# Cross-attention with heads of 64: products of 32 columns in place of 64, and the place of one weight in its pool

## The chip, the cores and the metric

The kernel runs on one core of a Trainium2 chip. The metric is device time in microseconds of one execution. Before the change three runs took 1196.61, 1198.14 and 1200.52 us: the median is 1198.14.

A core has a matrix engine (TensorE, here PE), three engines for elementwise work (VectorE or DVE, ScalarE or ACT, GpSimd or POOL), SyncE (SP), which mostly issues DMAs, and 16 DMA engines. Each engine runs its own instructions in order; semaphores order them among each other. A matmul takes a stationary operand (the "weights" that PE loads) and streams a moving one past it; it can be told to use the whole array of 128 rows by 128 columns, or a part of it. When only 64 or 32 columns are written, a 128-column product is issued as two or four matmuls[...].

## The reference

A decoder of two layers in fp32, on eight entries of 256 tokens with 256 features. The first layer is self-attention, cross-attention with heads of 16, and experts with Sinkhorn routing; the second is self-attention, a cross-attention with a null key and value, and experts with token routing beside a shared expert. The change lies in the second layer's cross-attention. For each of eight entries b it computes, with 16 heads of 64 and a context of 256 tokens of 512 features:

```
q = norm(x) Wq            k, v = ctx Wkv
e = exp(q k / 8)          n = exp(q null_k / 8)
out = (e v + n null_v) / (sum e + n)  Wo
x   = x + norm(out)
```

After it the routed experts need scores, which are one more product of the normed rows, with a router of 8 columns (E = 8). The shared expert is a gated feed-forward network: its first and third weights (`ws13`) make the hidden layer, its second (`ws2`) brings it back.

## The kernel before

Two helpers make a 128x128 block of a product: `product` (line 274) as two matmuls of 64 columns, `product4` (line 280) as four of 32 (`HP` is 32, `XD` 64, `P` 128). `product4` was in use in the first layer and in self-attention, whose heads are 16 wide. Each fp32 matmul shows as two MATMUL and two LDWEIGHTS records in the profile. All row and column forms are written there as rows x columns, so `128*64` is a matmul of 128 rows and 64 columns.

The second cross-attention (`null_cross_attention`, from line 1288) is a loop over b, about 59 us for each entry, from about 486 to 971 us of the span. The body of b first works through the attention itself (`weighted`): for pairs of 128-feature blocks, two heads to a block, scores `stx` (line 1431, 64 rows x 128 columns), their exponential `pTx` on ACT, and a sum of its two halves, `both`, on POOL (line 1437). PE takes the sums over the context with a 0/1 matrix (`den`, line 1446, 32 columns) and the weighted values `ox` (line 1470, 64 columns). The order on PE is: scores of the next pair, `den` of the pair before, `ox` of this one.

Then the projections of entry b+1 are made. Keys, values and queries (`k7`, `v7`, `q7` in `seven`, line 1346 on) are each a 2x2 block product in seven in place of eight multiplications, with sums of weights and rows made on DVE. For the first entry, the queries come from plain products (`features`, line 1293). Their steps are interleaved by hand, in the tuple of generators at line 1607, with the last sums of b (`rest`), the division by the sums (`reciprocals`, which goes through DRAM by SP's queue as `rd` and `rs`; `divide`), and the output product of b (`outward`, line 1529: `wo` and two norms). Then come the routing scores of b-1 (`sc`, `routed_scores`, line 1203) and the null key of b+1 (`nps`, line 1415). The norm of b+1 and of b-1's routed rows (`lnmv`, `lnve`, `lnrs`, `xn`, `xne`) runs on DVE and POOL, and their transposes on PE (line 291).

PE's order is written by hand from the projections on; the order on DVE, ACT and POOL is decided by a scheduler as the program is built.

The last entry (b = 7) has no next one. It closes the pool of the cross-attention's weights and opens a pool `mids` in the same place, on the right side of SBUF, for the shared expert: `load_shared` (line 1054) places `ws13`, two hidden buffers, then `ws2` from the lowest address up. `ended` (line 1033) sets the unused rows of a buffer's last part to zero on POOL. SP issues the load of `ws13` (lines 1028 and 1029, `ws<-L_ffn_ws_DF`) and later that of `ws2` (lines 1039 and 1040, `ws<-L_ffn_ws_FD`), and PE starts the shared expert's hidden products `hx` (line 1079) in the places where the projections stood before.

The routed experts (`token_experts`, from 971 us) use `product` for their hidden layer and output.

Of the kernel before, what the change touches and what calls it, by code (L numbers as in the profile page):

```python
# [29 lines left out]
F32 = mybir.dt.float32  # L30
# [9 lines left out]
P = 128  # L40
B, S, D = 8, 256, 256
NT = B * S // P
H, HD = 16, 16
HP = 32
CTX = 512
XH, XD = 16, 64
# [4 lines left out]
NFC = len(FCH)  # L51
# [106 lines left out]
def plain(  # L158
# [119 lines left out]
        ]  # L278

    def product4(out, lhsT, rhs, start, stop):  # L280
        for h in range(0, P, HP):
            nc.tensor.matmul(  # L282
                out[h : h + HP], lhsT[:, h : h + HP], rhs, start=start, stop=stop, skip_group_check=True
            )

    def transposed(rows, work, mm, tag, dst=None, bufs=2):

# [492 lines left out]
    nc8 = XH // 2  # L780
# [244 lines left out]
    def w_in(pool, src1, src3, name):  # L1025

        t = pool.tile([P, 2, 2 * FF + tail], F32, name=name, tag=name)
        nc.sync.dma_start(t[:, :, :FF], src1.rearrange("(c p) f -> p c f", p=P))
        nc.sync.dma_start(t[:, :, FF + tail :], src3.rearrange("(c p) f -> p c f", p=P))
        nc.gpsimd.tensor_copy(t[:, :, FF : FF + tail], t[:, :, 2 * FF :])  # L1030
        return t

    def ended(t):

        nc.gpsimd.memset(t[tail:, full, :], 0.0)
        return t
# [10 lines left out]
    shared = {}  # L1047
# [5 lines left out]

    def load_shared(pool):

        shared["ws13"] = w_in(pool, a["L1_ffn_ws1_DF"], a["L1_ffn_ws3_DF"], "ws13")

        shared["mid_s"] = [ended(pool.tile([P, NFC, 2 * S], F32, name=f"mid{i}")) for i in range(2)]
        shared["ws2"] = ended(pool.tile([P, NFC, D], F32, name="ws2"))

    def hidden(mid, first, n, pair, silu):

# [139 lines left out]
    def routed_scores(b):  # L1202

        ps = mm.tile([P, 2, D], F32, tag="mm", name="sc")
        for t in range(2):
            for c in range(2):
                product(
                    ps[:, t, :E], shared["xnT"][:, c, bass.ts(2 * b + t, P)], shared["router"][:, c, :], c == 0, c == 1
                )
        nc.vector.tensor_copy(sc[:, 2 * b : 2 * b + 2, :], ps[:, :, :E])  # L1210
# [77 lines left out]
    def null_cross_attention(phase):  # L1288
# [4 lines left out]
        def features(dst, w, rows, copy):  # L1293
            n = w.shape[1]
            for c2 in range(0, nc8, 2):
                ps = mm.tile([P, 2, S], F32, tag="mm", name="fm")
                for i in range(2):
                    for cc in range(n):
                        product(
                            ps[:, i, :], w[:, cc, (c2 + i) * P : (c2 + i + 1) * P], rows[:, cc, :], cc == 0, cc == n - 1  # L1300
                        )
                copy(dst[:, c2 : c2 + 2, :], ps)
# [43 lines left out]
        def seven(name, s_terms, t_terms, dst, tokens_first):  # L1346

            n = t_terms[0].shape[1]
            xy = scp.tile([P, 2, 2 * S], F32, tag="sc", name=name)
            xb, yb = xy[:, 0], xy[:, 1]  # L1350

            read = {id(xb): [], id(yb): []}

            def reads(bank, ins):
                read[id(bank)].append(ins)
                return ins

            def product_of(which, bank, fresh):

                s, t = s_terms[which - 1], t_terms[which - 1]  # L1360
                for i in range(1 if tokens_first else 4):
                    for c in range(n):
                        if tokens_first:
                            args = bank, s[:, c, :], t[:, c, :]
                        else:
                            args = bank[:, bass.ts(i, P)], t[:, c, bass.ts(i, P)], s[:, c, :]
                        for made in product(*args, fresh and i == 0 and c == 0, c == n - 1):
                            for other in (xb, yb):
                                for ins in read[id(other)] if other is not bank else ():
                                    tc.declare_no_dep(made.ins, ins.ins, reason="another bank")  # L1370

            if tokens_first:

                def of(i, j):
                    return dst[:, i, 8 * j : 8 * j + 8, :]

                def seen(bank):
                    return bank.rearrange("p (h d) -> p h d", h=8)

            else:  # L1380

                def of(i, j):
                    return dst[:, 4 * j : 4 * j + 4, bass.ts(i, P)]

                def seen(bank):
                    return bank.rearrange("p (c t) -> p c t", c=4)

            def kept(bank, what):
                t = work.tile([P, 2 * S], F32, tag="pT", name=f"{name}{what}", bufs=4)
                reads(bank, nc.scalar.copy(t, bank))  # L1390
                return seen(t)

            product_of(1, xb, True)
            p1 = kept(xb, "p")
            yield
            zb = mm.tile([P, 2 * S], F32, tag="mm", name=f"{name}z")
            product_of(2, zb, True)
            nc.vector.tensor_tensor(of(0, 0), p1, seen(zb), ALU.add)
            product_of(5, yb, True)
            p5 = kept(yb, "v")  # L1400
            yield
            product_of(6, xb, False)
            u = kept(xb, "u")
            yield
            product_of(7, xb, False)
            reads(xb, nc.vector.tensor_tensor(of(1, 1), p5, seen(xb), ALU.add))
            yield
            product_of(3, yb, False)
            reads(yb, nc.vector.tensor_tensor(of(0, 1), u, seen(yb), ALU.add))
            yield  # L1410
            product_of(4, xb, False)
            nc.scalar.copy(of(1, 0), seen(xb))
            yield

        def null_key(xnT):
            nps = mm.tile([P, 2, S], F32, tag="mm", name="nps")
            for k in range(2):
                product(nps[:, 0, :], wn[:, k].rearrange("p g w -> p (g w)"), xnT[:, k, :], k == 0, k == 1)
            en = work.tile([P, S], F32, tag="en", name="en")
            nc.scalar.activation(en, nps[:, 0, :], AF.Exp, scale=scale)  # L1420
            return en

        def weighted(kT, v, qT):
# [36 lines left out]
            for c2 in range(0, nc8, 2):  # L1460
                now = ahead
                if c2 + 2 < nc8:
                    ahead = block(c2 + 2)
                for i, both in enumerate(before):
                    sums(c2 - 2 + i, both)
                o = mm.tile([P, 2, S], F32, tag="mm", name="ox")
                for i, (pT, _) in enumerate(now):
                    for kt in range(2):
                        for g in range(2):
                            nc.tensor.matmul(  # L1470
                                o[XD * g : XD * (g + 1), i, :],
                                v[:, kt, 2 * (c2 + i) + g, :],
                                pT[:, g, kt, :],
                                start=kt == 0,
                                stop=kt == 1,
                                skip_group_check=True,
                            )
                (nc.vector.tensor_copy if c2 % 4 else nc.scalar.copy)(oT[:, c2 : c2 + 2, :], o)
                before = [both for _, both in now]
# [49 lines left out]
        def outward(b, oT, en):  # L1529
            y = work.tile([P, 2, D], F32, tag="y", name="yx", bufs=1)  # L1530
            ps = mm.tile([P, 2, D], F32, tag="mm", name="wo")
            for t in range(2):
                cols = bass.ts(t, P)
                product(ps[:, t, :], en[:, cols], nvw, True, False)
                for c in range(nc8):
                    product(ps[:, t, :], oT[:, c, cols], wout_x[:, c, :], False, c == nc8 - 1)
            nc.scalar.copy(y, ps)
            mv, rs = norm_stats([y[:, t, :] for t in range(2)], 1e-6, small, "lx")
            for t in range(2):
                xt = x[:, 2 * b + t, :]  # L1540
                normed(y[:, t, :], y[:, t, :], mv, rs, t)
                nc.vector.tensor_tensor(y[:, t, :], y[:, t, :], lns, ALU.mult)
                nc.vector.tensor_tensor(y[:, t, :], y[:, t, :], lnb, ALU.add)
                nc.gpsimd.tensor_tensor(xt, xt, y[:, t, :], ALU.add)
# [17 lines left out]
        en = null_key(xnT)  # L1562
# [5 lines left out]
        for b in range(B):  # L1568
# [31 lines left out]
            if b == 1:  # L1600
                in_range()
            if not more:
                w_out(shared["ws2"], a["L1_ffn_ws2_FD"])
                routing_tables(late)
            if more:

# [1251 lines left out]
```

## Time and profile before

| | us |
|---|---|
| three runs | 1196.61, 1198.14, 1200.52 |
| profiled execution, its own time | 1198.71 |
| its span | 1197.0 |
| PE busy / PE's weight loads | 1135.5 / 706.5 |
| DVE / ACT / POOL busy | 566.2 / 447.5 / 417.6 |
| `ox`, PE busy (512 records) | 62.3 |
| `wo`, PE busy (512 records) | 58.0 |
| `den`, PE busy (256 records) | 21.3 |

The span is the profiled execution from its first to its last instruction. Busy times of an engine add up the durations of its instructions; PE's weight loads are shown apart, since they overlap matmuls. [...] how long a group really holds PE is seen from its start to the start of the next group. A number in brackets at the end of a timeline's line is idle time before the group, and what ended it. PEclk is the clock that PE was granted, where 1.00 is full speed.

### The profile page before, as it was taken

Reading aid. Unit: us, or ns where it says so; the run is one execution under the profiler, and the core shown is the slowest. Engines: PE = TensorE matmul, PEld = TensorE weight load, DVE = VectorE, ACT = ScalarE, POOL = GpSimd, SP = SyncE. Lnnn points to the kernel's source line nnn. Section 1 sums busy time; section 2 is a strip of 40 time slices with the busy share of each in tenths; the row PEclk is TensorE's granted clock in tenths of the full one; section 3 lists DMA queues with packets and bytes.
Section 4 is the critical chain, followed back from the end, with each engine's and each line's share of the span. In section 5 each row is a group of like instructions: output and inputs, shape, how many; then the busy total and the mean of one; then the engine's idle time right before and its main releaser. Section 6 shows DMA issues by size and latency. Waiting matters only on the chain.

```text
span 1197.0 us, 31939 instructions
## 1 busy us (share of the span) xinstructions
PE 1135.5 (95%) x13788; PEld 706.5 (59%) x13788; DVE 566.2 (47%) x1564; ACT 447.5 (37%) x696; POOL 417.6 (35%) x482
## 2 busy tenths in 40 slices
PE   6898899998899999999999999999998999999996
PEld 2334444454445454666676767666664576888864
DVE  5465878778685643824241424242324473222213
ACT  3666665665443541314141414141413230222220
POOL 3245365455655730314141414141415114100013
PEclk9999999999999999999999999999998999999999
DMA  7046232130200600020202010101103007799924
GB/s 226 1 133 204 91 119 92 54 122 2 84 2 17 233 3 19 2 54 2 54 2 54 6 50 10 46 19 37 24 15 105 5 30 305 277 414 394 392 73 129
DMA packets 51446, 116.78 MB, mean 98 GB/s; under 512 B 8272, under 2 KB 36416, under 8 KB 46944
## 3 DMA queue, kind: packets, MB, share of 16 engines
q1 hardware_dynamic: 45120, 98.90, 24.0%
q0 software_dynamic: 3456, 12.73, 2.9%
q10 hardware_dynamic: 2720, 3.02, 0.7%
q8 instruction: 110, 1.80, 0.6%
q14 instruction: 40, 0.33, 0.1%
HBM read 104.00 MB, written 27.93 MB: 110 GB/s over the span
## 4 chain that ended last, share of the span: by engine, by line
PE 76%; POOL 7%; issue 6%; DVE 6%; ACT 4%; DMA 1%; SPq 0%; POOLq 0%; ACTq 0%; DVEq 0%
PE h L276 7%; PE k L276 6%; PE v L276 6%; PE wo L276 5%; PE ox L1470 5%; PE stx L1431 5%; PE st L334 4%; PE out L1846 4%; PE o L371 3%; PE out L1663 3%; PE h L1079 3%; PE qk L282 3%; PE q L276 3%; ACT pT L345 2%; PE den L1446 2%
## 5 line engine op out<-in xcount | busy, mean ns | idle before, releaser
L345 ACT ACTIVATE pT<-st 128x1024 f32<-128x1024 f32 (+1 forms) x128 | 110.7, 919 | 64.3 <-PE st L334 64.3
L371 PE MATMUL o<-pT,padv 128*32 128x256 f32 (+1 forms) x1536 | 99.7, 370 | 4.3 <-POOL pT L350 4.2
L371 PEld LDWEIGHTS o<-pT,padv 128*32 128x32 f32 x1536 | 40.6, 109 | 86.2 <-issue 37.5
L1437 POOL TENSOR_TENSOR both<-pTx 128x512 f32<-128x512 f32 x64 | 81.2, 1296 | 29.0 <-ACT pTx L1435 23.8
L276 PE MATMUL h<-xrT,w 128*64 128x128 f32 (+1 forms) x1936 | 87.0, 250 | 0.4 <-issue 0.4
L276 PEld LDWEIGHTS h<-xrT,w 128*64 128x64 f32 x1936 | 84.4, 137 | 3.3 <-issue 1.1
L345 ACT ACTIVATE pT<-st,kbias 128x1024 f32<-128x1024 f32 x64 | 67.9, 1112 | 44.0 <-PE st L334 44.0
L258 POOL TENSOR_TENSOR lnrs<-lnve,mhalf 128x2 f32<-128x2 f32 x48 | 34.7, 723 | 127.8 <-DVE lnve L256 124.1
L1072 DVE TENSOR_TENSOR midr<-sl,h 128x128 f32<-128x128 f32 x102 | 29.4, 288 | 102.5 <-PE h L276 69.9
L1435 ACT ACTIVATE pTx<-stx 128x1024 f32<-128x1024 f32 x64 | 62.1, 1022 | 40.8 <-PE stx L1431 27.7
L1071 ACT ACTIVATE sl<-h 128x128 f32<-128x128 f32 (+1 forms) x114 | 35.4, 311 | 94.7 <-PE h L276 55.7
L334 PE MATMUL st<-qm,kT 32*128 32x512 f32 (+1 forms) x512 | 66.8, 591 | 4.0 <-ACT pT L345 2.0
L1431 PE MATMUL stx<-qTx,kTx 64*128 64x256 f32 x512 | 64.4, 391 | 2.5 <-ACT pTx L1435 2.5
L282 PE MATMUL qk<-l_wqkv,xnT 128*32 128x512 f32 x512 | 63.3, 607 | 0.7 <-ACT xnT L294 0.7
L1470 PE MATMUL ox<-pTx,vx 128*64 128x256 f32 x512 | 62.3, 385 | 0.0
L258 POOL TENSOR_TENSOR lxrs<-lxve,mhalf 128x2 f32<-128x2 f32 x8 | 5.6, 706 | 159.9 <-DVE sc L1210 124.2
L1525 POOL TENSOR_TENSOR oT<-oT,rs 128x512 f32<-128x512 f32 x30 | 37.3, 1273 | 65.0 <-DMA rs<-rd 65.0
L1431 PEld LDWEIGHTS stx<-qTx,kTx 64*128 64x128 f32 x512 | 46.1, 186 | 20.3 <-ACT pTx L1435 7.2
L276 PE MATMUL wo<-wout_x,oT 128*64 128x256 f32 x512 | 58.0, 379 | 0.0
L350 POOL TENSOR_SCALAR_AFFINE_SELECT pT<-pT 128x512 f32<-128x512 f32 x64 | 42.0, 670 | 41.8 <-ACT pT L345 38.7
L1846 PE MATMUL out<-w,midr 128*64 128x256 f32 x408 | 47.1, 379 | 2.7 <-issue 2.7
L1470 PEld LDWEIGHTS ox<-pTx,vx 128*64 128x64 f32 x512 | 33.9, 136 | 26.4 <-issue 12.5
(361 smaller groups left out, 2164.1 us busy)
## 6 DMA issues: line engine op xcount, KB each, us to landing
w<-packs SPq DMA_DIRECT2D x22, 1408.0 KB
w<-packs SPq DMA_DIRECT2D x22, 768.0 KB
rs<-rd SPq DMA_DIRECT2D x16, 512.0 KB
packs<-L_ffn_w_eDF SPq DMA_DIRECT2D x8, 704.0 KB
packs<-L_ffn_w_eDF SPq DMA_DIRECT2D x8, 640.0 KB
packs<-L_ffn_w_eFD SPq DMA_DIRECT2D x8, 640.0 KB
ctxT<-ctx_T SPq DMA_DIRECT2D x8, 512.0 KB
wkv_x<-L_xattn_Wkv POOLq DMA_DIRECT2D x1, 4096.0 KB
```

What stands on the lines that cost most here:

```text
L258: nc.gpsimd.tensor_tensor(rs[:, :n], ve[:, :n], mhalf[:, :n], ALU.pow)
L276: nc.tensor.matmul(out[h], lhsT[:, h], rhs, start=start, stop=stop, skip_group_check=True)
L282: nc.tensor.matmul(out[h : h + HP], lhsT[:, h : h + HP], rhs, start=start, stop=stop, skip_group_check=True)
L334: nc.tensor.matmul(st[:, r, :, :n], self.kT[rows, c, bass.ts(kt, P)], self.qm[rows, :, c, q0:], start=True, stop=True,)
L345: nc.scalar.activation(pT[:, :, :, :n], st[:, 2 * k : 2 * k + 2, :, :n], AF.Exp, scale=self.scale, **kb)
L350: nc.gpsimd.affine_select(out=pT[:, :, :, :P], in_=pT[:, :, :, :P], compare_op=ALU.is_ge, fill=0.0, base=0, pattern=[[0, 2], [0, 2], [1, P ...
L371: nc.tensor.matmul(o[HP * j : HP * j + HP, m, q0:], self.v_pad[:, kt, 8 * c + 2 * j + m, :], pTs[j // 2][:, j % 2, m, : S - q0], start=kt ...
L1431: nc.tensor.matmul(st[:, g, kt, :], kT[rows, c, bass.ts(kt, P)], qT[rows, c, :], start=True, stop=True)
L1435: nc.scalar.activation(pT, st, AF.Exp, scale=scale)
L1437: nc.gpsimd.tensor_tensor(both, pT[:, :, 0, :], pT[:, :, 1, :], ALU.add)
L1470: nc.tensor.matmul(o[XD * g : XD * (g + 1), i, :], v[:, kt, 2 * (c2 + i) + g, :], pT[:, g, kt, :], start=kt == 0, stop=kt == 1, skip_group ...
L1846: nc.tensor.matmul(ps[h], mid[:, i, h], sets[k % len(sets)][1][:, i, :], start=i == 0, stop=i == NFC - 1, skip_group_check=True,)
```

## The change

`product4` returns the list of its matmuls, as `product` did. `product4` replaces `product` in the second cross-attention: in `features`, in the seven products of keys, values and queries, in the null key, in `outward`, and in `routed_scores`. The weighted values `ox` are issued as four matmuls of 32 columns where they were two of 64. `product` stays for the routed experts. Apart from that, `ws2` is taken first in the pool `mids`, so that it is at the lowest address and `ws13` above it; the `ended` for `ws2` moves from its allocation to just ahead of its load. Lines from 282 on are two higher afterwards.

```diff
     def product4(out, lhsT, rhs, start, stop):
-        for h in range(0, P, HP):
+        return [
             nc.tensor.matmul(
                 out[h : h + HP], lhsT[:, h : h + HP], rhs, start=start, stop=stop, skip_group_check=True
             )
+            for h in range(0, P, HP)
+        ]
...
     def load_shared(pool):
+        shared["ws2"] = pool.tile([P, NFC, D], F32, name="ws2")
         shared["ws13"] = w_in(pool, a["L1_ffn_ws1_DF"], a["L1_ffn_ws3_DF"], "ws13")
         shared["mid_s"] = [ended(pool.tile([P, NFC, 2 * S], F32, name=f"mid{i}")) for i in range(2)]
-        shared["ws2"] = ended(pool.tile([P, NFC, D], F32, name="ws2"))
...
     def routed_scores
-                product(
+                product4(
                     ps[:, t, :E], shared["xnT"][:, c, bass.ts(2 * b + t, P)], shared["router"][:, c, :], c == 0, c == 1
...
         def features
-                        product(
+                        product4(
...
         def seven, product_of
-                        for made in product(*args, fresh and i == 0 and c == 0, c == n - 1):
+                        for made in product4(*args, fresh and i == 0 and c == 0, c == n - 1):
...
         def null_key
-                product(nps[:, 0, :], wn[:, k].rearrange("p g w -> p (g w)"), xnT[:, k, :], k == 0, k == 1)
+                product4(nps[:, 0, :], wn[:, k].rearrange("p g w -> p (g w)"), xnT[:, k, :], k == 0, k == 1)
...
         def weighted
-                        for g in range(2):
+                        for at in range(0, P, HP):
                             nc.tensor.matmul(
-                                o[XD * g : XD * (g + 1), i, :],
-                                v[:, kt, 2 * (c2 + i) + g, :],
-                                pT[:, g, kt, :],
+                                o[at : at + HP, i, :],
+                                v[:, kt, 2 * (c2 + i) + at // XD, at % XD : at % XD + HP],
+                                pT[:, at // XD, kt, :],
...
         def outward
-                product(ps[:, t, :], en[:, cols], nvw, True, False)
+                product4(ps[:, t, :], en[:, cols], nvw, True, False)
                 for c in range(nc8):
-                    product(ps[:, t, :], oT[:, c, cols], wout_x[:, c, :], False, c == nc8 - 1)
+                    product4(ps[:, t, :], oT[:, c, cols], wout_x[:, c, :], False, c == nc8 - 1)
...
             if not more:
-                w_out(shared["ws2"], a["L1_ffn_ws2_FD"])
+                w_out(ended(shared["ws2"]), a["L1_ffn_ws2_FD"])
```

## The prediction

> **What bounds the kernel now.** I read first the busy time of each engine and the chain that ended last, on the profile's page:
>
> ```profile
> PE 1135.5 (95%) x13788; PEld 706.5 (59%) x13788; DVE 566.2 (47%) x1564; ACT 447.5 (37%) x696; POOL 417.6 (35%) x482
> ...
> PE 76%; POOL 7%; issue 6%; DVE 6%; ACT 4%; DMA 1%; SPq 0%; POOLq 0%; ACTq 0%; DVEq 0%
> ```
>
> TensorE is the bound. An average hides stages, so next came the windows: one cross-attention entry (b=2), then a stretch of the last one. Columns: window, length, busy time (instructions) of PE, PEld, DVE, ACT, POOL, granted clock, DMA share, GB/s.
>
> ```profile
> 605.00:664.00 59.00, 58.68 (x658) 40.03 (x658) 20.03 (x51) 17.90 (x27) 19.40 (x21) 1.00 0.11 28
> 919.90:926.50 6.60, 6.52 (x8) 2.52 (x8) 3.03 (x6) 0.00 (x0) 0.29 (x1) 0.54 0.93 261
> ```
>
> In the stage that the change edits PE is all but never free, at full clock; a microsecond taken out of PE's stream there is a microsecond of the end. But "busy" includes what a matmul loses at its start, so I measured starts against starts in the timeline of PE (start, busy time, line, operands, number):
>
> ```profile
> 611.39 1.95 PE L1470 MATMUL ox<-pTx,vx 128*64 128x256 f32 x16
> 613.27 2.00 PE L1431 MATMUL stx<-qTx,kTx 64*128 64x256 f32 x16
> 615.19 0.64 PE L1446 MATMUL den<-both,hot 128*32 128x256 f32 x8
> 615.76 1.95 PE L1470 MATMUL ox<-pTx,vx 128*64 128x256 f32 x16
> 617.64 0.64 PE L1446 MATMUL den<-both,hot 128*32 128x256 f32 x8
> ...
> 621.11 1.97 PE L276 MATMUL k<-ctxT,wkv_x 128*64 128x128 f32 x32
> 623.01 0.64 PE L1446 MATMUL den<-both,hot 128*32 128x256 f32 x8
> 623.58 1.97 PE L276 MATMUL k7z<-ctxT,wkv_x 128*64 128x128 f32 x32
> 625.37 1.81 PE L276 MATMUL k<-sw,tw 128*64 128x128 f32 x30
> ```
>
> The same timeline of the earlier cross-attention, which already works in 32 columns:
>
> ```profile
> 439.45 3.64 PE L282 MATMUL fm<-ctxT,wkv_x 128*32 128x256 f32 x64
> 443.01 0.71 PE L334 MATMUL st<-qm,kT 32*128 32x256 f32 x8
> ...
> 444.55 1.05 PE L282 MATMUL ao<-l_wo,attT 128*32 128x256 f32 x16
> 445.41 3.64 PE L282 MATMUL fm<-ctxT,wkv_x 128*32 128x256 f32 x64
> 448.86 0.62 PE L371 MATMUL o<-pT,padv 128*32 128x128 f32 x16
> 449.30 1.05 PE L282 MATMUL ao<-l_wo,attT 128*32 128x256 f32 x16
> ```
>
> Inside one shape: 64 columns of 256 take 0.108 us a record (`wo`: 3.45 for 32), of 128 0.0546 (`k`: 1.75 for 32). In 32 columns, 256 take 0.0539 (`ao`: 445.41 - 444.55 = 0.86 for 16; `fm`: 448.86 - 445.41 = 3.45 for 64), 128 take 0.0275 (`o`: 0.44 for 16). A 128x128 product is half as many records of twice the length: same time. Where the shape changes it isn't: `ox` then `stx` or `den` is 1.88 where 16 x 0.108 = 1.73 is due, +0.15; `den` then `ox` 0.57 where 8 x 0.0539 = 0.43 is due, +0.14; `k` then `den` 1.90 for 1.75, +0.15; `den` then `k7z` +0.14. From 32 columns to 32 rows, `fm` then `st`, 3.56 for 3.45: +0.11. From 32 to 32 columns: nothing.
>
> [...] here 32 records of `lg` (32 columns of 8) take 0.27 us, 8.6 ns each[...] the window above shows 0.54 after 3.42 us of idleness. [...] the trace has 1.69 us for two `xne` beside POOL's `both`, 0.74 with POOL idle.
>
> **The change part by part.** (1) `ox`, the seven products `k7`, `v7`, `q7`, `wo`, the null key and `fm` of b=0 go to 32 columns: twice the records, each half as long, 0 in themselves; the number of waits in the instructions is the same. (2) What goes is the shape changes against `den`, which is 32 wide. In each b: `den` then `ox` three times, `ox` then `den` once, `k` then `den` once, `den` then `k7z` once: 6 x 0.145 = 0.87. Three `ox` then `stx`, and transposes, stay, at 0.11 for 0.15: 0.11. The first `k7z` group itself takes 1.79 for 1.75: 0.04. (3) `sc`: 16 records of 64 columns of 8 take 0.55 us (start to start, 600.11 to 600.66); at the 8.6 ns of `lg`, 32 take 0.27: 0.28, in each b from 1 on (b-1's scores).
>
> Sum for an entry: 0.87 + 0.11 + 0.04 + 0.28 = 1.30.
>
> (4) What eats it. Sc copies and the last norm chain shift in DVE's order, and from b=1 to 5 POOL takes `lnrs`, `lnrs`, then `both`, where before it took `lnrs`, `both`, `lnrs`, `both`. The first `den` of b=2 already started late: it needs the second `both`, which ended at 610.76 (POOL: `lnrs` to 607.45, `both` to 608.70, `lnrs` to 609.55, `both` to 610.76). With the new order, `lnrs` ends about 606.7, the two `xne` with POOL idle 0.75, `lnve` 0.16, `lnrs` 0.70, two `both` 2.5: 610.8. So this `den` stays where it was, and of the 0.40 saved ahead of it (0.28 at `sc`, some 0.12 at the smaller shape changes), I count half as lost to a wait for `both`: 1.1 for b=2 to 5 (4.4), 0.9 for b=1, where the order changes too, 1.0 for b=0 (no `sc`). b=6 keeps POOL's order: 1.29; b=7 about 1.2. Total 0.9 + 1.0 + 4.4 + 1.3 + 1.2 = 8.8 us.
>
> Costed at nothing, with cover: faster `ox` asks sooner for `pTx` and `both`, which have over 1 us of slack in the middle of an entry; PE's total wait on `pTx` from 486 to 900 is 2.2 us. `oT`'s last division by the sums ends at 639.6 and `wo` reads it at 649.7: 10 us. The 32-wide weight loads run beside matmuls (PEld 40.03 of 59.00). The routed experts keep 64 columns.
>
> (5) `ws2` lowest in its pool. The last entry shows the wait that it might concern:
>
> ```profile
> 915.49 0.40 SPq L1028 DMA_DIRECT2D ws<-L_ffn_ws_DF  x1
> ...
> 919.98 6.62 PE L1079 MATMUL hx<-xnTe,ws 128*128 128x512 f32 x8 [3.42 <-DMA ws<-L_ffn_ws_DF]
> ```
>
> The load of `ws13` leaves right after the last `ox` (914.80), and PE waits for it 3.42 us, then runs 8 records in 6.55 where 8 x 0.43 = 3.43 is due: 3.1 more through the clock. By the addresses, `ws13` overlapped `vx`, which `ox` reads; afterwards `ws2` does, and `ws13` lies on `wkv_x` alone. But in both built programs the wait of `ws13`'s load is still on the last `ox`: the pool's first writer takes on the waits of the pools closed before it. SP's queue behind it (`rd`, `ws2`, `rs`) has the same order. I take 0. Both ends: 0, and -6.5 if it does leave early. What does move is the phase: the wait ends at the transfer's landing, which follows the last `ox` whatever came before, so PE's 3.42 stays.
>
> The profiled execution took 1198.71 us around a span of 1197.0; less 8.8 that is 1189.9 around 1188.2. It lies 0.6 above the median of the runs (1198.14), so the median should be 1189.3; I say 1189.5.
>
> **Rivals.** *A, the other side: narrow records hit a floor.* `k7` and `q7`, with 128 elements a record, leave 27.3 ns per 32-wide record. For: 64-wide records of 64 elements (`h`, 176 in 5.13 us) come no faster than 29.1 ns; if a record, and not the width of its weights, sets that, each loses 1.8 ns: 672 per b, 7 times, 4704 x 1.8 = 8.5 us, and the time is about 1198, no change. At 31 ns it is 17 us: 1206, slower. It decides the sign from about 29.2 ns on. Against: `o` runs 27.5 ns, `lg` 8.6 ns, both 32-wide, though in bursts of 16 and 32 only; 64-wide `sc` shows 59 ns for each pair of columns' loads, so `h`'s floor is that of a 64-wide load.
> *B, POOL late.* If the two `xne` still meet `both` (1.69 instead of 0.75) the first `den` of b=2 to 5 is 0.95 later: -3.8 of the gain, 1193. [...]
> *C, `ws13` leaves early after all*: 6.5 more, 1183. Against: the built waits.
> *D, no cost at the shape changes, only modelled ends*: then nothing is gained, 1198; against it, differences of starts, which aren't modelled, show it.
>
> **How the numbers follow.** Main case 0.66 (1186 to 1193: 8.8 give or take three, as the slow-clock stretch and the runs' spread of 1196.61 to 1200.52 move it). A without change 0.08, A slower 0.07, B 0.10, C 0.06, D 0.03. 0.3% is 3.6 us, about what a measurement of this kernel can tell from no change: faster below 1194.5, slower above 1201.7. Faster: main, C, most of B: 0.80; same: D, most of A's first part and the rest of B: 0.12; slower: A's second part and a little of its first: 0.08. The range from 1184 to 1198.5 holds the main case but for its tails (0.62), B, most of A without change and D (0.10), and is cut through C: some 0.84. Cases of both signs don't share it evenly; the main case's own range stands above.
>
> **What would show it.** Right: `den` to `ox` 0.43, `ox` to `den` and `k` to `den` 1.73 to 1.76, `sc` 0.27, entries near 58.0 instead of 59.1 us, PE still waiting 3.4 us at the last entry's `hx`. Wrong: `k` groups over 1.8 us (A); the first `den` later than before against its own `stx`, on POOL's `both` (B); `ws` landing before the last `ox` (C).

## The result and the profile after

The changed kernel takes 1201.59 us (median of 8 runs, 1198.66 to 1203.56) against 1197.38 for the kernel before in the same comparison: a ratio of 1.0031, 95% interval 1.002 to 1.0042. It is slower by some 4 us, where 8.8 us less was forecast. The profiled execution took 1203.56 around a span of 1201.8; it is the slowest of the eight, so stages are compared below, not spans.

The profile after, from its page: busy times, the chain that ended last, and the queue that brings instructions.

```profile
PE 1133.2 (94%) x17876; PEld 708.3 (59%) x17876; DVE 560.8 (47%) x1564; ACT 447.8 (37%) x696; POOL 418.6 (35%) x482
...
q8 instruction: 142, 2.33, 0.8%
...
PE 71%; POOL 9%; DVE 7%; issue 7%; ACT 4%; DMA 1%; SPq 0%; POOLq 0%; DVEq 0%; ACTq 0%
```

PE is busy for 2.3 us less while the span is longer: PE waits more. `issue`, time in which an engine waited for nothing that the profile shows, went from 6% of the chain to 7%. The line in the middle counts packets, MB and share of time. Before the change it read:

```profile
q8 instruction: 110, 1.80, 0.6%
```

PE's 8,176 additional records came in 32 additional fetches: 0.53 MB / 32 = 16 KB, some 256 records for each. Such a packet of 256 instructions is called a page below.

The windows show where PE waits (columns as in the prediction): the first entry, then b=3, of the kernel after.

```profile
486.00:545.00 59.00, 57.10 (x1172) 38.87 (x1164) 26.96 (x45) 16.56 (x23) 17.36 (x14) 1.00 0.12 29
663.00:722.00 59.00, 57.26 (x1160) 40.13 (x1152) 17.96 (x47) 17.98 (x26) 19.67 (x20) 1.00 0.12 30
```

Before, PE was busy for 58.36 and 58.68 us of these. The clock is at full speed in both. PE's waits from 486 to 990 us, in the view of waits (total, times, longest, in us), after:

```profile
PE k L282 <- issue: 6.4, 6, 1.8
PE hx L1081 <- DMA ws<-L_ffn_ws_DF: 3.5, 1, 3.5
PE stx L1433 <- ACT pTx L1437: 2.5, 8, 0.3
PE q L282 <- DVE qTx L1408: 0.4, 1, 0.4
```

The first line is new; the wait at `hx` is as long as before (3.4). The six waits are inside groups of key products, and PE's timeline shows one:

```profile
515.45 1.93 PE L282 MATMUL k<-sw,wkv_x 128*32 128x128 f32 x64
517.20 1.49 PE L282 MATMUL k<-ctxT,tw 128*32 128x128 f32 x47
519.93 0.73 PE L282 MATMUL k<-ctxT,tw 128*32 128x128 f32 x17 [1.24 <-issue]
520.39 1.99 PE L282 MATMUL v7z<-wkv_x,ctxT 128*32 128x512 f32 x16
```

Between the 47th and the 48th record of one group, with no semaphore between them, 1.51 us pass from start to start where 0.027 is normal. All six together, from start to start, are 7.9 us too long: 1.49, 2.02, 1.49, 0.73, 1.17 and 0.99 in b=0, 1, 3, 4, 5 and 6. b=2 has none. Counted in all records of PE, weight loads and the sequencer's own among them, the restarts stand 2304, 4864, 2304, 2560 and 2304 apart: 9, 19, 9, 10 and 9 x 256. PE stops at the ends of its pages.

What keeps the page away is seen in the DMA queues. From 512.2 to 517.2 us and in the 2 us after it, with packets, MB and share:

```profile
q1 hardware_dynamic: 155, 1.05, 94.2%
```

```profile
q8 instruction: 1, 0.02, 3.8%
q1 hardware_dynamic: 5, 0.00, 0.3%
```

The first 5 us are the two transfers `rs<-rd`, 512 KB each; no instruction packet begins in them. The page that ran out at 518.4 lasted 3.5 us of `k` (128 pairs of a weight load and a matmul at 27.3 ns), so PE entered it near 514.9, in the middle of `rs<-rd`. By the trace's packets, the fetch before had begun at 510.35, 0.2 us after PE entered a page. The next one, due near 515, began only at 517.28, some 2.4 us after PE had entered its page, behind `rs<-rd`, and PE went on at 519.93, 2.65 us after that. For the six stalls, the fetch began 2.1 to 2.8 us after PE entered the page, and from its start to PE's next record 2.61 to 2.92 us passed. A page of `k` lasts 3.5 us, so by these numbers a fetch can start no more than 0.6 to 0.9 us late before PE runs dry. At 64 columns a page of `k` lasts 7.0 us (128 pairs at 54.6 ns), and PE did not stop.

### The profile page after: what moved, and what is told of

Read it like the earlier page. It is cut to its first block, busy times and chain, and to the rows that moved or that the text cites. A ratio compares the mean times of both kernels' runs of the same rounds, so it can differ in the third digit from the quotient of the medians.

```text
span 1201.8 us, 40110 instructions
## 1 busy us (share of the span) xinstructions
PE 1133.2 (94%) x17876; PEld 708.3 (59%) x17876; DVE 560.8 (47%) x1564; ACT 447.8 (37%) x696; POOL 418.6 (35%) x482
## 4 chain that ended last, share of the span: by engine, by line
PE 71%; POOL 9%; DVE 7%; issue 7%; ACT 4%; DMA 1%; SPq 0%; POOLq 0%; DVEq 0%; ACTq 0%
PE v L282 7%; PE h L276 7%; PE k L282 6%; PE wo L282 5%; PE ox L1472 4%; PE st L336 4%; PE out L1848 4%; PE o L373 3%; PE h L1081 3%; PE out L1665 3%; PE qk L282 3%; PE stx L1433 3%; ACT pT L347 2%; PE q L282 2%; PE fm L282 2%
## 5 line engine op out<-in xcount | busy, mean ns | idle before, releaser
L1472 PE MATMUL ox<-pTx,vx 128*32 128x256 f32 x1024 | 63.0, 380 | 0.0
L282 PE MATMUL wo<-wout_x,oT 128*32 128x256 f32 x1024 | 58.2, 379 | 0.0
L1480 DVE COPY oT<-ox 128x512 f32<-128x512 f32 x16 | 11.1, 691 | 81.2 <-PE ox L1472 81.2
```

The costliest lines, as they stand in the source:

```text
L282: nc.tensor.matmul(out[h : h + HP], lhsT[:, h : h + HP], rhs, start=start, stop=stop, skip_group_check=True)
L1472: nc.tensor.matmul(o[at : at + HP, i, :], v[:, kt, 2 * (c2 + i) + at // XD, at % XD : at % XD + HP], pT[:, at // XD, kt, :], start=kt == 0 ...
```

## The experiments

The theory after the result (F): instructions for narrow products are fetched too late, because their fetch waits behind `rs<-rd`. The rival (R): records of 128 elements in 32 columns run dry by themselves. A third part (P, Q) concerns what else is missing from the gain. Beside the time, each run gives the length of seven entries, from the first `stx` of b=0 to that of b=7. The start and the end of the kernel don't enter it: the profiled executions differ by 2.3 us (475.38 and 477.66) when the first null key begins, and up to there the code is the same. The seven entries took 413.01 before and 417.02 after: +4.0 of the 4.2 by which the medians differ. The kernel before was timed again beside each group of runs (medians from 1197.38 to 1198.87), so the ratios compare better than the times. Stalls are counted in the one execution that was profiled.

| run | us | ratio to before, 95% | seven entries, us | stalls in `k`, us |
|---|---|---|---|---|
| changed kernel | 1201.59 | 1.0031 (1.0020 to 1.0042) | 417.02 | 7.9 |
| rs_late | 1193.01 | 0.9955 (0.9939 to 0.9971) | 408.73 | 0 |
| before_rs_late | 1198.91 | 1.0003 (0.9991 to 1.0015) | 412.98 | 0 |
| before_ox32 | 1193.15 | 0.9960 (0.9948 to 0.9973) | 408.89 | 0 |
| no_ws2 | 1199.60 | 1.0017 (1.0004 to 1.0031) | 415.90 | 6.8 |
| late_pool | 1190.78 | 0.9925 (0.9900 to 0.9950) | 405.89 | 0 |
| late_pool_q | 1188.88 | 0.9917 (0.9897 to 0.9937) | 404.03 | 0 |
| rs_twice | 1202.87 | 1.0040 (1.0026 to 1.0054) | 416.05 | 7.0 |
| before_sc32 | 1197.08 | 0.9988 (0.9978 to 0.9998) | 412.80 | 0 |
| page_shift | 1201.99 | 1.0038 (1.0018 to 1.0059) | 414.37 | 5.4 |
| rs_ahead | 1217.78 | 1.0157 (1.0132 to 1.0183) | 433.31 | 15.5 |
| before_seven32 | 1206.42 | 1.0072 (1.0049 to 1.0096) | 419.76 | 5.7 |
| before_pool_q | 1197.63 | 0.9994 (0.9980 to 1.0008) | 411.00 | 0 |

**The transfer out of the way.** In `reciprocals`, the two `rs<-rd` move into a function, `spread`, that is called later, behind a copy of one element:

```diff
-                for made in (k7, k7, v7, k7, k7, k7, v7, v7, q7, v7, q7, v7, v7, q7):
+                for n, made in enumerate((k7, k7, v7, k7, k7, k7, v7, v7, q7, v7, q7, v7, v7, q7)):
                     next(made)
+                    if n == 4:
+                        nc.vector.tensor_copy(rs[:1, 0, :1], kT[:1, 4, :1])
+                        spread()
...
```

> The changed kernel, but the two transfers `rs<-rd` (512 KB each) of b=0 to 6 leave only after the sixth of the seven key products has been added (one VectorE copy of a single element from kT into rs ahead of them). Theory F (fetch): PE's next page of instructions waits behind `rs<-rd`; the stalls of 1.5, 2.0, 1.5, 0.7, 1.2 and 1.0 us in the k groups go, 7.9 us in all: near 1193.7, faster than before. Rival R (a rate): narrow matmuls of 128 elements run dry by themselves, whatever is being transferred: stalls stay, near 1201.6. A slip of the output product `wo` behind the later division would show as a wait of `wo` on POOL or DVE: not expected, 10 us of slack against some 4 us of delay.

> The kernel before, with the same delay of `rs<-rd`. Theory F: at 64 columns a page of instructions lasts twice as long and no fetch was late, so nothing is won: within 1 us of before. If the delay itself is worth something or costs something (another order on VectorE, the later division), it shows here: rival R gives no number of its own, also 0.

The six stalls are gone, and the time is 1193.01, 0.7 us below what F said; R falls. The same group in PE's timeline, with the late transfer:

```profile
517.30 1.93 PE L282 MATMUL k<-ctxT,tw 128*32 128x128 f32 x64
519.05 1.90 PE L282 MATMUL v7z<-wkv_x,ctxT 128*32 128x512 f32 x16
```

It wasn't done quite as written. The copy holds back only the half of `rs` with its element; in b=0 one transfer still ran near 513 to 515.5, and the other from 519 on. The fetch that fell into the first began at 515.81, some 0.8 us after PE had entered its page near 515.0, and that was early enough, in keeping with the 0.6 to 0.9 us above. So half of the transfer at the old time does no harm, which F allows and hadn't said. In the kernel before, the delay brings nothing: 412.98 for seven entries against 413.01.

**More transfer ahead of the fetch.** First as a second pair behind the first (`rs_twice`), then as a pair into DRAM ahead of it (`rs_ahead`, whose edit is shown):

```diff
+            spare = dram.tile([2, XD, nc8 * S], F32, name=f"spare{b}")
+            for g in range(2):
+                nc.sync.dma_start(
+                    spare[g], rd[g : g + 1].rearrange("g c q -> g (c q)").to_broadcast([XD, nc8 * S])
+                )
             for g in range(2):
                 nc.sync.dma_start(
...
```

> The changed kernel with the two transfers `rs<-rd` each made twice, the same rows to the same place, at the early time: 10 us of transfer in place of 5. Theory F: the fetch of a page waits until they are through, so each stall grows by up to 5 us, and b=2, which has none now, gets one of about 3: 20 to 36 us more, between 1221 and 1238, with the stalls again at the ends of pages of 256 records and ended some 2.7 us after the fetch begins. Rival R: the stalls belong to narrow records; doubling a transfer that nothing waits for (10 us of slack at `wo`) adds nothing: 1201.6.

> The changed kernel with two more transfers of the same 512 KB each, from `rd` to an unused place in DRAM, issued ahead of the two `rs<-rd`, so that 10 us of transfer stand in the queues when PE asks for a page (doubling `rs<-rd` itself put the second pair behind the fetch, since it waits for the first to land). Theory F: each late fetch is later by the time of that pair, 3.5 to 5 us: the stalls add up to 28 to 39 us in place of 7.9, b=2 among them with 1.7 to 3.2; the time is near 1222 to 1233. Rival R: near 1201.6.

The first was a miss: 1202.87, with the stalls where they were and no longer. The second pair writes the same rows, so SP issued it only from 514.15 on, as the first landed. PE had entered its page near 513.2, before that, and the fetch began at 515.61 without waiting for the second pair, whose packets run until 521.5. That says that a fetch waits for what was queued ahead of it, not for all that is under way. With the other pair ahead, the time rises to 1217.78, 16.2 above the changed kernel; R is out again. F's size was too high: 28 to 39 us of stalls were expected and 15.5 came, in four entries (3.4, 3.6, 4.4 and 4.1 in b=0, 1, 3 and 5). The fetch in b=0 began at 518.64, while the last packets of `rs` ran until 521.1, so about 7 us of the pairs stood before it and not 10; why it did not wait for all of them stays open; and in b=2 it began at 647.16, but the page in hand reached into the slower `v`. The time rose by more than the stalls, and the windows show why: the stall of b=0 (about 518 to 521.3) and then the 1.3 us after it.

```profile
517.90:521.30 3.40, 0.31 (x11) 0.04 (x3) 0.00 (x0) 0.00 (x0) 0.00 (x0) 0.98 0.54 116
521.30:522.60 1.30, 1.25 (x21) 1.13 (x25) 0.00 (x0) 0.00 (x0) 0.97 (x1) 0.50 0.00 0
```

After 3.1 us without work PE goes on at a granted clock of 0.50, and so it does after the other three (3.4 to 4.1 us without work), for 3.2, 5.5, 2.7 and 5.6 us in turn. Half of that is 8.5 us; with the 7.6 us that the stalls have grown by it comes to 16.1, and the seven entries are 16.3 us longer. The stalls of the changed kernel, at most 1.8 us without work, did not lower the clock: it was 1.00 from 481.2 to 924.8 us.

**Pages shifted.** 128 more records before the first entry, so that pages end elsewhere (the comment is added here):

```diff
-            for k in range(2):
+            for k in (0, 1) * reps:        # reps is 5 for b=0
                 product4(nps[:, 0, :], wn[:, k].rearrange("p g w -> p (g w)"), xnT[:, k, :], k == 0, k == 1)
```

> The changed kernel with the first null key made five times over, ahead of entry b=0: 32 more matmuls, which are 128 more records on PE, half a page of 256, and nothing else moved. Theory F: pages now end half a page later against the transfers `rs<-rd`. With a page's request at each 256th record, a fetch that can begin only after `rs<-rd` where the request falls into it, and 2.7 us from its begin to use, the k groups of b=2, 4 and 6 stall, by 1.9, 1.4 and 1.0 us, and those of b=0, 1, 3 and 5, which stalled by 1.5, 2.0, 1.5 and 1.2, do not: 4.3 us in place of 7.9. The extra products cost some 3.5 us at full clock and up to 7 at half: the time itself near 1201 to 1205. Rival R: the same groups stall as before, by the same amounts.

The stall of b=2, which had none, is 1.81 us:

```profile
634.39 1.04 PE L282 MATMUL k<-ctxT,tw 128*32 128x128 f32 x29
637.00 1.17 PE L282 MATMUL k<-ctxT,tw 128*32 128x128 f32 x34 [1.56 <-issue]
```

b=4 has 0.97, b=6 has 1.29, b=1 and 3 none, as said; against it b=0 and b=5 keep 0.58 and 0.75 where none was expected. Together 5.4 us for 4.3 expected and 7.9 before. The seven entries are 2.65 us shorter than with the change; the stalls lost 2.5 of that. Neither `k` nor its operands were touched: where a stall falls is set by the count of records ahead of it.

**Parts alone.** The weighted values, and the seven products:

```diff
 before_ox32
-                        for g in range(2):
+                        for at in range(0, P, HP):
...
 before_seven32
-                        for made in product(*args, fresh and i == 0 and c == 0, c == n - 1):
+                        for made in product4(*args, fresh and i == 0 and c == 0, c == n - 1):
```

> The kernel before, with only the weighted values `ox` in 32 columns. Shape changes that go: three `den` to `ox` and one `ox` to `den` for each b, 0.14 to 0.15 us each, and 0.04 at each of three `ox` to `stx`: 0.7 for each of 8 entries, 5.6 us; less up to 0.15 in b=1 to 5 where the first `den` is late on POOL anyway: 4.9 to 5.6 faster than before, near 1192.2, with no stall in the k groups, since a record of `ox` still takes 54 ns. Rival: the shape changes are not what was measured, and 32 columns bring nothing: 1197.4.

> The kernel before with only the seven products of keys, values and queries in 32 columns; `ox`, `wo`, `sc` and the null key stay at 64. Theory F: these alone bring the late fetches, 4 to 10 us by where the pages fall, and the loss of `den` on POOL, about 0.46 in b=2 to 5; they win `k` to `den` and `den` to `k7z`, 0.34 each entry, and pay a shape change at `wo`, `sc` and the null key against `q`, up to 5 times 0.14 each entry. 7 x (0.7 - 0.34) + 1.8 + 7 = 11: slower, between 1203 and 1211. If the width itself were at fault and not the fetch, the rival gives the same sign, so the stalls' places decide: at page ends, after a fetch that follows `rs<-rd`.

`ox` alone wins 4.85 us (the interval of the ratio gives 3.2 to 6.2), as the prices of the shape changes said: entries of 58.54 for 59.12. The seven products alone lose 8.3, with the stalls again at page ends (5.7 us, in b=0, 1, 2, 3 and 6):

```profile
641.50 1.39 PE L282 MATMUL k<-ctxT,tw 128*32 128x128 f32 x42 [1.54 <-issue]
```

**The place of `ws2`.**

```diff
-        shared["ws2"] = pool.tile([P, NFC, D], F32, name="ws2")
         shared["ws13"] = w_in(pool, a["L1_ffn_ws1_DF"], a["L1_ffn_ws3_DF"], "ws13")
...
+        shared["ws2"] = ended(pool.tile([P, NFC, D], F32, name="ws2"))
...
```

> The changed kernel with `ws2` back above `ws13` in its pool, its zeroing back at its allocation. The wait of the load of `ws13` is for the last `ox` either way: same as the changed kernel within 1 us, 1201.6, and PE waits about 3.5 us at `hx` in both. Rival: the place of `ws2` brought something that the stalls hide: then slower than the changed kernel by up to 6.5 us.

PE's wait at `hx` is 3.5 us with either place, so the move brings nothing there. The time was 2.0 below the changed kernel's (1.7 by the ratios), more than the 1 us expected; the intervals of the two ratios overlap, and the entries differ by 1.1 us, as do the stalls. So the rival's loss of up to 6.5 us without the move is out; why the stalls are a little shorter stays open.

**The rest of the gain: POOL and `sc`.** After the change, the first `den` of b=2 to 5 starts with its operands late. In PE's timeline of b=3:

```profile
673.28 1.09 PE L1448 MATMUL den<-both,hot 128*32 128x256 f32 x6
673.97 0.42 PE L1472 MATMUL ox<-pTx,vx 128*32 128x256 f32 x2
674.20 0.39 PE L1448 MATMUL den<-both,hot 128*32 128x256 f32 x2
674.21 2.10 PE L1472 MATMUL ox<-pTx,vx 128*32 128x256 f32 x30
676.24 2.00 PE L1433 MATMUL stx<-qTx,kTx 64*128 64x256 f32 x16
```

From `den` to the next `stx` 2.96 us pass, where 0.43 + 1.87 would do. POOL shows why (its timeline, with idle time in brackets):

```profile
669.13 0.70 POOL L258 TENSOR_TENSOR lnrs<-lnve,mhalf 128x2 f32<-128x2 f32 x1 [0.21 <-DVE lnmv L254]
669.89 0.19 POOL L1196 COPY rstd<-lnrs 128x2 f32<-128x2 f32 x1
670.76 0.69 POOL L258 TENSOR_TENSOR lnrs<-lnve,mhalf 128x2 f32<-128x2 f32 x1 [0.68 <-DVE lnve L256]
671.41 3.74 POOL L1439 TENSOR_TENSOR both<-pTx 128x512 f32<-128x512 f32 x3
```

It idles 0.68 us for the second `lnve`, which stands behind the two `xne` on DVE, and both `both` come behind that. Before and after the change, the first `q` behind `sc` starts just after DVE's sum `qTx` ends. In b=2 of the kernel after, PE and DVE:

```profile
662.74 0.46 PE L282 MATMUL sc<-router,xnTe 128*32 128x8 f32 x32
663.32 1.08 PE L282 MATMUL q<-xnT,twq 128*32 128x128 f32 x32
```

```profile
662.61 0.65 DVE L1408 TENSOR_TENSOR qTx<-q7v,q 128x512 f32<-128x512 f32 x1
```

The sum ends at 663.26, 0.06 us ahead of `q`. Two orders were changed in turn, on POOL and then on DVE too (the comments are added here):

```diff
-                    xe = routed_norm(b - 1, work)
+                    with tc.issue_after(summed[1].ins):     # the second both, on POOL
+                        xe = routed_norm(b - 1, work)
...
-                next(q7), next(q7)
+                next(q7)
+                with tc.issue_after(added[-1].ins):         # qTx<-q7v, on DVE
+                    finish()                                # the norm of the output rows
+                next(q7)
```

> The changed kernel with the late `rs<-rd`, and on POOL the rows of `routed_norm` (mean, its `lnrs`, rstd) queued behind the second `both` of an entry. Theory P: what is left of the loss in b=2 to 5 is the first `den`, which waits for the second `both`, behind two `lnrs` on POOL; from the first `den` to the third `stx` it takes 2.95 us where 2.30 would do: 0.65 in four entries, some 0.2 in b=1 and 6: 3.0 less than with the late transfer alone, near 1190.0. Rival: POOL's order is covered and something else holds `den`: no gain, 1193.0.

> As the run before it, and on VectorE the statistics `lxst` of the output rows queued behind the sum `qTx` of the seventh query product. Theory Q: the products after `sc` wait for that sum, not for `sc` (0.58 us from `sc` to `q` in 32 columns, 0.55 in 64); with the sum first, that becomes some 0.3: 0.27 in each of 7 entries, 1.9 less, near 1188.1. Rival: `sc` itself takes 0.55 in either width: 0.58 stays, and nothing is won.

> The kernel before with only the routing scores `sc` in 32 columns. The prediction's step (3): 0.28 us in each of 7 entries, 2.0 faster than before, near 1195.8. Theory Q: `q` after `sc` waits for VectorE's sum `qTx`, so the time from `sc` to `q` stays at 0.55 to 0.6: the same as before, 1197.6.

> The kernel before, all at its old widths, with the two orders of the run late_pool_q on POOL and VectorE. It tells what of that run's 10 us is the orders' and not the columns'. The first `den` of b=1 to 5 waits 0.17 now: 0.9. `q` after `sc`: if it waits for `qTx` at 64 columns too, 0.1 to 0.27 in 7 entries, and none if 16 records of 64 columns really take 0.55. Between 0.9 and 2.8 us faster than before: 1195.2 to 1197.1 against 1198.

With `both` first, entries 2 to 5 go from 58.7 to 58.05, 0.65 as expected, and the time is 1190.78. With the sum `qTx` ahead of `lxst` as well, all of b=2 to 6 are 57.77, and the time is 1188.88. PE's timeline in that kernel, from the end of b=2 and the beginning of b=3:

```profile
658.09 0.44 PE L282 MATMUL sc<-router,xnTe 128*32 128x8 f32 x31
658.36 0.29 PE L282 MATMUL q<-xnT,twq 128*32 128x128 f32 x1
...
668.35 0.64 PE L1450 MATMUL den<-both,hot 128*32 128x256 f32 x8
668.81 1.91 PE L1474 MATMUL ox<-pTx,vx 128*32 128x256 f32 x32
```

From `sc` to `q` are 0.27 us, 8.9 ns a record; the changed kernel has 0.58 there, with the same records. `sc` did not set that time; the sum `qTx` did. With `sc` in 32 columns alone, `q` again starts 0.06 us after that sum, and an entry is 0.05 us shorter. The time of that run (0.9978 to 0.9998) would allow the 2.0 us of the prediction's step as well as next to nothing; it is the entries, 0.2 us shorter in seven, that speak against the step. In the kernel before, the two orders take 0.31 from each entry (59.12 to 58.81, seven entries 2.0 less); the times alone, 0.9994 with an interval over 1 and a median above the 1195.2 to 1197.1 expected, can't tell that from nothing. There, `sc` takes 0.44 at 64 columns. So of the 9.0 us that late_pool_q wins in seven entries, 2.0 belong to the orders at any width; with the same orders, the columns are worth 7.0, once the transfer is out of their way. This kernel is faster than both.

## Why the prediction was wrong

The forecast was 1189.5 (1184 to 1198.5), faster; the kernel came out at 1201.59, slower.

- What bounds the kernel: right, PE all but without pause (58.68 us busy of 59.00) at full clock (1.00) in that stage. It is what made each stall cost its full length.
- Step (1), twice the records at half the length: the step that failed. In the array it holds: 27.3 ns a record in every `k` group between stalls, 53.9 in `ox`, half of the 54.6 and 108 at 64 columns. "0 in themselves" left out that each record has to be brought. The products on PE were counted, the bytes of instructions weren't, though the profile's page has a line for their queue. 7.9 us went there in the profiled execution: PE stood still at the ends of pages whose successor was fetched late, behind `rs<-rd`.
- Step (2), the shape changes: right, but for the small part at `ox` to `stx` (1.88 to 1.86, where 1.84 was due). `den` to `ox` went from 0.57 to 0.43, `k` to `den` from 1.90 to 1.77, `k7z` from 1.79 to 1.75; `ox` alone was worth 4.85 us where 4.9 to 5.6 were due.
- Step (3), `sc`, 0.28 an entry: wrong. The 0.55 us from `sc` to `q` were read as the price of 16 records; they ended with the sum `qTx` on DVE. Worth 0 (0.55 before, 0.58 after), until that sum was put first.
- Step (4), POOL: the mechanism was right, the size was off. Half of 0.40 was set aside; the first `den` of b=2 to 5 waits for 0.65 us, where it had waited for 0.18 (2.63 from `den` to `stx`, of which 0.57 + 1.88 are due): 0.47 more. The chain that was worked out, from the end of the first `lnrs` to that of the second `both`, came as put down: 4.08 us in b=2 for 4.11, POOL's idle time behind the two `xne` included. But the first `lnrs` ended only 0.28 us earlier against the entry's first `stx` (4.63 after it, 4.91 before the change), where 0.75 was put down (606.7 for 607.45).
- Step (5), `ws2`: right, 3.5 us of wait at `hx` with either place.
- The rivals: A had the groups and, by chance, nearly the sum (8.5 us), but not the cause. Its test, `k` groups over 1.8 us, came true in six entries, by one stall each and not by a slower rate. B's sign came true, the first `den` later on POOL's `both`, but not its cause: the two `xne` ran in 0.73 us with POOL idle and did not meet `both`. C and D did not happen.

With 7.9 for step (1), 0.28 x 7 for step (3) and 0.27 x 4 for step (4), the forecast of 1189.5 comes to 1200.4, 1.2 below the measured time. The entry without a stall, b=2, shows the same without step (1): 0.41 shorter than before, where 1.1 was forecast, of which 0.28 and 0.27 are the two steps' part; 0.14 stay open.

## What to carry to other kernels

Here, splitting products into narrower matmuls cost nothing in the array (in `k` two records of 27.3 ns for one of 54.6) and doubled their instructions. Before counting on such a split, work out how long a page of 256 instructions lasts in the densest stretch (here 3.5 us) and which large transfers run in that stretch. What is left of the page after the time from a fetch's start to its use (here 2.6 to 2.9 us) is all that a fetch can be held up: 0.8 us did no harm here, 2.1 us and more emptied PE. If a transfer can hold it up for longer, move the transfer rather than the products. And a time from one group's start to the next's is the group's price only if nothing else ends it: look for an engine whose last write comes just ahead of the next start (here `qTx`, 0.06 us ahead of `q`).

## What the runs showed of the hardware

- PE's instructions come in packets of 16,384 bytes (110 of them before the change, 142 after it), some 256 records each. One packet that began some 2.4 us after PE had entered a page of 3.5 us left PE without work for 1.24 us. It began at 517.28; none had begun since 510.35, and PE went on at 519.93.
- From the start of such a late packet to PE's next record 2.6 to 2.9 us passed in the changed kernel, while the packet itself took 1.2 to 1.35.
- The fetch was held up by transfers queued ahead of it (two more transfers of 512 KB ahead: stalls of 3.4 to 4.4 us, `rs_ahead`) and not by those issued after PE had entered the page (`rs_twice`: the fetch began at 515.61, the second pair ran until 521.5). It did not wait for all of what was ahead: in b=0 of `rs_ahead` it began at 518.64, 2.4 us before the last of it had run.
- Routing scores of 8 columns run at 8.9 ns a record in 32 columns (31 in 0.27 us, `late_pool_q`), and 16 records of 64 columns in 0.44, 27 ns each (`before_pool_q`).
